# A fused four-layer graph kernel: four engines issue in the order of emission

## The chip, the cores and the metric

The kernel runs on one core of a Trainium2 chip, in fp32. Times are device microseconds from the start to the end of one launch. Three runs of the kernel before gave 2439.32, 2439.52 and 2441.19 us; the median is 2439.52 us. Lower is better.

## What is computed

The input x holds 128 graphs of 64 nodes with 256 features, and all share one 64 x 64 adjacency. Four layers follow each other, each with a residual and a layer norm:

```python
x = _layernorm(x + _L0_gnn_ref(x, adj, ...))   # A_hat x, 256->512, batch norm, relu, 512->256, batch norm
x = _layernorm(x + _L1_gnn_ref(x, adj, adj, ...))
x = _layernorm(x + _L2_gnn_ref(x, adj, ...))
x = _layernorm(x + _L3_gnn_ref(x, adj, W, a))  # graph attention: softmax over masked scores, times x W
```

Layer 0's two batch norms run over all 8192 rows, so nothing behind one can start before all rows are through what is ahead of it. Layer 1 is a Chebyshev step whose Laplacian is scaled by its largest eigenvalue, then a masked attention with 4 heads and an MLP with an exact gelu, with three affine layer norms. Layer 2 is two graph convolutions, then an LSTM over windows of 1, 2, 3 and 4 nodes, each rewriting some nodes of h:

```python
for p in range(1, MAX_SKIP + 1):
    wins = h[:, :nw * p, :].reshape(Bv * nw, p, Hd)
    last = _lstm_last(Wih[p - 1], Whh[p - 1], bih[p - 1], bhh[p - 1], wins)
    h = h.at[:, idx, :].set(last.reshape(Bv, nw, Hd))
```

## The kernel before, in words

**Tiles.** x is cut into 16 blocks of 8 graphs. A block is 4 tiles of 128 rows by 256 features, 128 x 1024 fp32. For each block there is one buffer with rows on the partitions (X[i]; x0 to x7 hold two blocks each) and one with features on the partitions (H[i]; h0 to h3 hold four each). Eight temporary buffers of a block's size (t0 to t7) and four PSUM buffers of two banks each (ps0 to ps3) are handed out and taken back by two stocks, `mem` and `PS`.

**The order of emission.** The kernel has a planner of its own, `flow` (L130). Each task is a Python generator which, ahead of every piece of work, yields the engine it needs and an estimate of its time ("T" for TensorE 3.45 us, "V" for VectorE 1.25, "S" for ScalarE 1.05, "G" for POOL 1.0, "Q" for a DMA), with the PSUM and temporary buffers it takes. `flow` keeps a model clock for each engine, picks the step that can start earliest, with margins and priorities of streams, and lets that task emit its instructions. So the order in which the program is written down is already a plan of the whole run. A step emits all its instructions together: the four tiles of a norm's statistics (L272, L273 for each tile, L274), or the eight operations of an affine norm's application (L297, L300 for each tile).

**The order of issue.** The program is written under a framework that tracks the tiles' dependencies, puts in the semaphores, and schedules: before the change, its scheduler is free to put each engine's instructions into another order than the one emitted, as long as dependencies hold.

**The stages.** The first `flow` runs layer 0: `first_block` (aggregation L322, L346, PSUM out L537, statistics), the batch norm's coefficients `bn_coeffs`, `second_block` (relu on ScalarE, L566, statistics), and beside them the largest eigenvalue by squaring a matrix again and again (L440 to L490; L468 is the squaring). Between the two flows stands set-up code: loads of weights on SP's queue (L855, L372, L862, and L381 for the biases bih and bhh), memsets on POOL, and on VectorE L870 and L873, `V.tensor_tensor(bl, bl, bh, ALU.add)`. The second `flow` (L1574) runs everything else in streams:
- `end_block` (L628 to L649), the end of layer 0: load of x on SP (L635), batch norm on ScalarE (L638), transposes on PE (L340, 128 x 128 each), residual from PSUM on VectorE (L646), layer norm. `ln_steps_act` (L301 to L316) does this norm: L272 to L274 on VectorE, the power -0.5 on POOL (L308), L311 on VectorE, then four L314 on ScalarE.
- `block`, layer 1: aggregation (L322), ScalarE copy L660, product with Wc (L358), PSUM out L669, an affine norm (`ln_affine_steps`, L286 to L300, with its power at L294), relu and residual L673, transposes L334, ScalarE copy L681, products L346 for q and k, the attention (VectorE L743 to L754, ScalarE L750) and the MLP.
- `gcn_block` and `lstm`, layer 2: L952 and L1024 are products on PE, L964 and L1104 gates from PSUM on ScalarE, L991 tanh on ScalarE, L983 and L830 products and sums on POOL, L1062 to L1100 moves and sums, L1222 to L1250 the graph convolution's evictions and relu.
- `last_block`, layer 3: L1364 copies on ScalarE, L1404, L1428, L1441 exponentials, L1450 to L1471 the weighted sums, L1161 to L1193 the last LSTM pieces beside them.

The streams overlap: block by block, layer 2 starts while layer 1 is under way, and layer 3 while layer 2's LSTM ends.

Of the kernel before, what the change touches and what calls it, by code (L numbers as in the profile page):

```python
# [33 lines left out]
def kernel(ctx: ExitStack, tc: tile.TileContext, a: dict, out: bass.AP):  # L34
    nc = tc.nc
    V, S, G, T = nc.vector, nc.scalar, nc.gpsimd, nc.tensor

    def bc_mid(ap, n):

        return ap.unsqueeze(1).to_broadcast([ap.shape[0], n, ap.shape[1]])  # L40
# [1595 lines left out]
```

## Time and profile before

| | |
|---|---|
| median of 3 runs | 2439.52 us (2439.32 to 2441.19) |
| the profiled execution | 2439.17 us |
| its span (first to last instruction) | 2437.4 us |
| granted TensorE clock, mean | 0.983 |
| DMA: bytes moved, share of 16 engines on the main queue | 57.47 MB, 6.9% |

A profile comes from one execution. PE is TensorE's matmuls, PEld its weight loads, DVE VectorE, ACT ScalarE, POOL GpSimd, SP the engine that issues the transfers (SPq in the lists). The page gives each engine's busy time first, then the span in 40 slices, a digit for the busy tenths of each; PEclk is the clock that the throttle granted PE, in tenths of full speed. Lists of waits name the waiting instruction, then the releaser: "PE ps L334 <- DVE t L673" is a matmul of line 334 into a PSUM buffer that waited for VectorE's line 673. In a timeline a line is: start, duration (both in us), engine, line, operation, output<-input, and in brackets the engine's idle time ahead of it with its releaser. In windows each engine's busy time in a stretch is followed by its number of instructions in brackets, then the mean clock, DMA share and GB/s. Lines are those of the kernel before.

### The profile page before, as it was taken

To read this page: it belongs to the slowest core of one execution; us is meant where nothing else is said; L and a number is where in the kernel's file an instruction comes from. 1 tells how busy PE (TensorE), PEld (TensorE's weight loads), DVE (VectorE), ACT (ScalarE), POOL (GpSimd) and SP (SyncE) were. 2 spreads that over 40 slices of the span, in tenths; PEclk is the share of its full clock that TensorE was granted. 3 is DMA by queue.
4 is the path that set the end of the run, shared out by engine and by line. 5 is a ranking of instruction groups with operands and counts; after the bars stand their busy time and mean duration, and the time that the engine had idled before them with its cause. 6 is when DMAs were issued, how large, how long until landed. Compare 5 with 4: busy or idle time off the path is not lost. (4 is left out here: it accounts for less than half of the span.)

```text
span 2437.4 us, 33965 instructions
## 1 busy us (share of the span) xinstructions
PE 2348.3 (96%) x13700; PEld 1798.9 (74%) x13700; DVE 1215.1 (50%) x2864; ACT 1169.9 (48%) x2138; POOL 566.7 (23%) x426
## 2 busy tenths in 40 slices
PE   8999889999999999999999999999999999998997
PEld 5544567766676666676676788899999888887785
DVE  4542377646475345744462433344435444455446
ACT  2255453543444444335544444444444654468766
POOL 0000034222333222422231221222212222122112
PEclk9999989999999999999999999999999999999998
DMA  5110111000000000000010000000001000001111
GB/s 172 44 52 0 40 31 49 27 9 10 1 10 18 10 9 10 1 10 34 20 61 1 18 1 1 1 18 1 1 1 35 1 9 10 18 27 66 40 35 44
DMA packets 40974, 57.47 MB, mean 24 GB/s; under 512 B 4592, under 2 KB 33904, under 8 KB 40816
## 3 DMA queue, kind: packets, MB, share of 16 engines
q1 hardware_dynamic: 39712, 54.22, 6.9%
q8 instruction: 107, 1.75, 0.3%
q10 hardware_dynamic: 1104, 1.08, 0.1%
q14 instruction: 51, 0.42, 0.1%
HBM read 38.52 MB, written 16.78 MB: 23 GB/s over the span
## 5 line engine op out<-in xcount | busy, mean ns | idle before, releaser
L1024 PE MATMUL ps<-x,x 128*128 128x256 f32 x1024 | 248.6, 380 | 0.7 <-DVE t L1092 0.7
L1024 PEld LDWEIGHTS ps<-x,x 128*128 128x128 f32 x1024 | 191.5, 190 | 26.4 <-issue 1.6
L314 ACT ACTIVATE x<-x,ln_nm,ln_rs 128x256 f32<-128x256 f32 x196 | 103.7, 592 | 97.0 <-DVE ln_nm L311 95.5
L1024 PE MATMUL ps<-t,x 128*128 128x256 f32 x576 | 141.0, 379 | 0.0
L308 POOL TENSOR_TENSOR ln_rs<-ln_rs,neghalf 128x4 f32<-128x4 f32 (+1 forms) x72 | 70.5, 980 | 231.1 <-DVE ln_rs L274 217.3
L1024 PEld LDWEIGHTS ps<-t,x 128*128 128x128 f32 x576 | 108.6, 190 | 14.6 <-issue 0.4
L346 PE MATMUL ps<-t,W1T 128*128 128x512 f32 x256 | 115.2, 593 | 0.0
L952 PE MATMUL ps<-h,wL 128*128 128x192 f32 (+2 forms) x504 | 111.6, 375 | 0.0
L952 PEld LDWEIGHTS ps<-h,wL 128*128 128x128 f32 x504 | 79.1, 190 | 27.6 <-issue 26.7
L272 DVE BATCH_NORM_STATS2 ln_st<-x 128x6 f32<-128x256 f32 x256 | 98.2, 404 | 0.5
L1100 ACT ACTIVATE t<-t,bih 128x512 f32<-128x512 f32 (+2 forms) x63 | 41.0, 652 | 107.6 <-DVE t L1090 105.9
L952 PE MATMUL ps<-h,x 128*128 128x256 f32 x384 | 86.8, 379 | 0.0
L964 ACT ACTIVATE t<-ps,bih 128x512 f32<-128x512 f32 (+3 forms) x104 | 61.5, 642 | 44.0 <-PE ps L952 43.9
L294 POOL TENSOR_TENSOR ln_rs<-ln_rs,neghalf 128x4 f32<-128x4 f32 x32 | 36.9, 1153 | 188.8 <-DVE ln_rs L274 188.6
L346 PEld LDWEIGHTS ps<-t,W1T 128*128 128x128 f32 x256 | 46.3, 190 | 46.4 <-issue 46.4
L952 PEld LDWEIGHTS ps<-h,x 128*128 128x128 f32 x384 | 72.9, 190 | 10.3 <-issue 0.5
L1083 DVE COPY t<-ps 128x256 f32<-128x256 f32 (+2 forms) x63 | 23.7, 378 | 113.5 <-PE ps L1024 113.5
L273 DVE BATCH_NORM_AGGREGATE ln_mv<-ln_st 128x2 f32<-128x6 f32 x448 | 71.3, 167 | 0.0
L346 PE MATMUL ps<-t,wA 128*128 128x512 f32 x144 | 67.9, 617 | 2.8 <-ACT t L681 2.8
L952 PE MATMUL ps<-t,wL 128*128 128x512 f32 x144 | 64.9, 607 | 2.5 <-ACT t L1250 2.5
L1090 DVE TENSOR_TENSOR t<-ps,t 128x512 f32<-128x512 f32 (+2 forms) x63 | 38.1, 604 | 54.8 <-PE ps L1024 47.9
L1100 ACT ACTIVATE x<-x,bih 128x512 f32<-128x512 f32 (+2 forms) x57 | 36.6, 641 | 55.7 <-DVE x L1090 55.4
(692 smaller groups left out, 5688.2 us busy)
## 6 DMA issues: line engine op xcount, KB each, us to landing
t<-in_x_dram SPq DMA_DIRECT2D x26, 512.0 KB, 3.9
xd<-x SPq DMA_DIRECT2D x16, 512.0 KB, 2.6
x<-xd SPq DMA_DIRECT2D x6, 512.0 KB, 3.3
out_dram<-x SPq DMA_DIRECT2D x6, 512.0 KB, 3.0
wL<-in_L_gnn_Wih_dram SPq DMA_DIRECT2D x2, 1024.0 KB, 4.9
h<-in_x_dram SPq DMA_DIRECT2D x4, 512.0 KB, 4.2
x<-in_L_gnn_Whh_dram SPq DMA_DIRECT2D x2, 1024.0 KB, 4.9
t<-xd SPq DMA_DIRECT2D x4, 512.0 KB, 3.3
```

Of the source, the lines that this page charges most:

```text
L272: V.bn_stats(st[:, t, :], y[:, t, :])
L273: V.bn_aggr(mv[:, t, :], st[:, t, :])
L294: G.tensor_tensor(rs, rs, neghalf[:, :NT], ALU.pow)
L308: G.tensor_tensor(rs, rs, neghalf[:, :n], ALU.pow)
L314: S.activation(y[:, t, :], y[:, t, :], AF.Identity, scale=rs[:, t : t + 1], bias=nm[:, t : t + 1])
L346: T.matmul(ps[:, c, :], w[:, k, (off + c) * P : (off + c + 1) * P], yT[:, k, :], start=(k == 0), stop=(k == nk - 1),)
L952: T.matmul(spread(fm(PS[ps])[:, j, :n], q), WL[p][0][:, k, m], x_of(0, q)[:, k], start=(k == 0), stop=(k == 1),)
L964: S.activation(of(sl)[:, j], fm(PS[ps])[:, j, :n], AF.Tanh if g == 2 else AF.Sigmoid, bias=bias(g, c))
L1024: T.matmul(dst, WS[p][name](k, g), y[:, k], start=first and k == 0, stop=k == 1, skip_group_check=not first)
L1083: V.tensor_copy(y[:, 1, :], v[:, 0, :])
L1090: V.tensor_tensor(y[:, 0:2, :], v[:, 2:4, :], y[:, 0:2, :], ALU.add)
L1100: S.activation(of(act[g])[:, 0], of(act[g])[:, 0], f, bias=bias(g, 0))
```

## The change

Two lines are put at the head of the kernel's function. They tell the framework that TensorE, VectorE, ScalarE and POOL issue their instructions in the order in which the program emits them. The transfers on SP's queue, and what the engines wait for among each other, stay with the framework. No instruction of the kernel's own is added, removed or altered, and `flow` emits the same order as before. In the kernel after, all lines stand two lower.

```diff
     nc = tc.nc
     V, S, G, T = nc.vector, nc.scalar, nc.gpsimd, nc.tensor
+    E = mybir.EngineType
+    ctx.enter_context(tc.manual_schedule(engines={E.PE, E.DVE, E.Activation, E.Pool}))
```

The built programs hold 69 loads of ScalarE's function table after the change and 73 before; these loads are put in by the compiler, where the function set of two successive activations differs.

## The prediction

> **What bounds the kernel now.** I read the busy times first, then the slices and the windows by stage, then PE's waits, then the timeline of single waits.
>
> ```profile
> PE 2348.3 (96%) x13700; PEld 1798.9 (74%) x13700; DVE 1215.1 (50%) x2864; ACT 1169.9 (48%) x2138; POOL 566.7 (23%) x426
> PE   8999889999999999999999999999999999998997
> PEclk9999989999999999999999999999999999999998
> ```
>
> PE is the bound, and its work is untouched. So only what PE loses can move: idle time (2437.4 - 2348.3 = 89 us, of which some 16 lie before its first and after its last matmul) and time at a lower clock. DVE and ACT at half of the span have slack on average. By stage (columns: length, then busy PE, PEld, DVE, ACT, POOL, granted clock):
>
> ```profile
> 150.00:350.00 200.00, 176.07 (x681) 95.30 (x681) 86.54 (x240) 116.35 (x174) 23.86 (x21) 0.92 0.07 20
> 500.00:600.00 100.00, 92.74 (x531) 64.83 (x530) 59.80 (x140) 40.73 (x57) 28.92 (x19) 0.93 0.03 11
> 960.00:1120.00 160.00, 150.95 (x1108) 107.26 (x1107) 100.00 (x213) 62.59 (x76) 57.36 (x32) 0.97 0.03 11
> 1200.00:1650.00 450.00, 449.92 (x2114) 371.44 (x2110) 192.85 (x359) 195.80 (x374) 108.45 (x74) 1.00 0.04 14
> 2180.00:2310.00 130.00, 116.53 (x767) 96.54 (x766) 75.24 (x253) 107.81 (x242) 25.44 (x28) 0.98 0.19 62
> 2380.00:2437.40 57.40, 40.28 (x276) 30.20 (x268) 33.92 (x150) 39.90 (x102) 13.04 (x20) 0.82 0.14 47
> ```
>
> From 1200 to 1650 nothing can be won: PE is busy throughout. The losses are single gaps in the other stages. The waits view (total, times, longest) names them; most occur once:
>
> ```profile
> PE ps L334 <- DVE t L673: 5.4, 1, 5.4
> PE ps L358 <- ACT h L964: 3.5, 1, 3.5
> PE ps L334 <- DVE t L1222: 3.4, 1, 3.4
> PE ps L340 <- ACT h L964: 3.4, 1, 3.4
> PE ps L346 <- ACT t L681: 2.8, 1, 2.8
> PE ps L952 <- ACT t L1250: 2.5, 1, 2.5
> ```
>
> A wait that names ACT L964 need not mean that ACT was slow. The timeline of ACT before the 3.4 us gap:
>
> ```profile
> 516.92 1.09 ACT L314 ACTIVATE x<-x,ln_nm,ln_rs 128x256 f32<-128x256 f32 x2 [4.30 <-DVE ln_nm L311]
> 517.92 0.61 ACT L991 ACTIVATE t<-h 128x512 f32<-128x512 f32 x1
> 518.44 1.08 ACT L314 ACTIVATE x<-x,ln_nm,ln_rs 128x256 f32<-128x256 f32 x2
> 519.42 1.24 ACT L964 ACTIVATE h<-ps,bih 128x512 f32<-128x512 f32 x2
> ```
>
> L964's input, PE's gate product, was finished at 514.73. ACT sat idle for 4.30 us, because an L314 that waited for a layer norm on DVE stood in front. The scheduler's order cost the gap, not ACT's speed. The granted clock is 0.50 from 519.47 to 526.30, just behind it.
>
> **What the skill says of it.** The Trainium skill, "TensorE: Matmul & The Clock Gate", table under "Why this matters for your kernels": PE gaps above some 3 us drop the clock to half; its section "What's actually happening" gives a window of 3.41 us that runs freely. The trace has the half-speed stretches in that unit (6.83 us behind 517.35 and 582.18, 3.41 behind 987.58, 1011.95 and 1096.3), but already behind a gap of 2.35 us, and none behind 1.75. I go by the trace: a removed gap of 2 us or more also pays back half of its stretch. The same skill, "PSUM — Partial Sum Buffer", "Engine vs sequencer instructions": ScalarE's, VectorE's and GpSimd's queues are strictly first in, first out. The ACT lines above agree, and the whole forecast rests on it: who stands in front decides.
>
> **The change, part by part.** It adds and removes no arithmetic. It fixes the order of four engines as the planner emits it; SP's 130 transfers stay with the scheduler. The two orders compared: PE keeps 6737 of 7236 instructions in place, DVE 959 of 2864, ACT 652 of 2077, POOL 107 of 431, SP 118 of 132. Four ACT table loads go (73 to 69; 1.28 us each in the chain of waits). All sums are against the profiled 2439.17 us (span 2437.4 and 1.8 around it), 0.35 below the median of 2439.52, which I ignore.
>
> 1. *Middle, 345 to 1200.* I followed each PE gap back through its releasers and asked which link the new order keeps. PE's own order there is unchanged. In each large case the instruction PE waits for was ready in time and no longer has the blocker in front:
> - 517.35 (3.37 us, above): L964 now ahead of L314.
> - 582.18 (3.47): L964 was ready at 578.64 but stood behind a tanh L991, which waited for POOL L983 behind POOL L830 (2.35 us).
> - 783.9 (1.61) and 892.2 (1.16): L1250 and L964 stood behind four L314 each.
> - 987.58 (3.42): DVE L1222 was ready at 984.54, behind L669 and L753 (1.22 us each) and a norm's statistics.
> - 1011.95 (2.53): DVE L1242 was ready at 1005.63, behind an affine norm.
> - 1093.5 and 1096.3 (0.76, 2.35): ACT L681 was ready at 1092.6, behind five L314.
> Sum 18.7 us, and small ones 2.4: 21.1. Half-speed stretches 2 x 6.83 + 3 x 3.41 = 23.9, half of that 11.9. Together 33. What takes a gap's place is the next-late operand, so I take 85%: **-28** (range -33 to -15).
>
> 2. *DVE in strict order, everywhere.* Step by step emission puts a consumer right behind its producer: 287 such neighbours before, 982 after (448 are L272 then L273, 128 are L297 then L300). In the trace a dependent neighbour costs 0.12 to 0.14 us more from start to start than an independent one (L273 0.22 against 0.08, L297 0.52 against 0.37). 695 x 0.125 = 87 us more on DVE, spread over a span where it idles 1220. This costs where DVE is dense: 650 to 700 goes from 43 to 48 of 50 us, 950 to 1000 from 46 to 51. There, and where the chain is a single norm (+0.5 us for stats, 3.2 to 3.9 for the eight affine operations), I take **+5** (0 to +15). Elsewhere PE's slack covers it: for each instruction that stands behind one it stood ahead of before, I compared its lateness with its slack to PE's use. From 345 to 1340 none is late beyond its slack by 0.4 us; from 1340 to 1990 only some seven are, by 0.4 to 1.1.
>
> 3. *Start of layer 1, 276 to 340.* In the old order the scheduler starts the second flow's work before the set-up that is emitted ahead of it; now DVE L873 (bl + bh) stands ahead of the first L646:
>
> ```profile
> 285.05 1.22 DVE L646 TENSOR_TENSOR x<-ps,t 128x1024 f32<-128x1024 f32 x1 [1.33 <-PE ps L340]
> 294.71 0.18 DVE L873 TENSOR_TENSOR bih<-bih,bhh 128x32 f32<-128x32 f32 x1
> 286.84 0.45 SPq L381 DMA_DIRECT2D bhh<-in_L_gnn_bhh_dram  x1
> ```
>
> bhh is issued at 286.84 behind six loads on SP's queue and lands 4.7 us later, at 291.5. All of DVE waits for that: +6.5 us on the first L646, and PE's second L340 with it. PE also loses the h3 transposes that the scheduler had pulled ahead as filler, and ACT does eight L314 before the L638 of h3. Followed by hand, PE reaches L334 of t6 at 320.7 instead of 313.65 (+7), and L346 of t7 at 341.7 instead of 337.28, since the gaps of 2.44 and 2.77 us at 331 and 334 mostly go. **+4.4** (0 to +10: a longer gap also stretches the half clock, 6.83 us behind 308).
>
> 4. *Small places.* First batch norm: one L468 moves ahead of L566, +0.8. From 1994 to 2002 the fillers move behind the chain L1450, L1452, L1460, L1471: +2.5; small gaps in 1663 to 2146 (4.4 in all), half gone: -2. SP's swaps cost nothing, as its DMA share is 3 to 7% there; without that cover, one landing (about 4 us). POOL's new order is costed within each chain.
>
> 5. *2186 to 2310.* ACT is dense (107.8 of 130). L1364 copies (1.07 us) and two table loads leave the chain at 2220 to 2232: -3.9; 2247: -1; 2305, with L1441 no longer split by two table loads: -1.9 and -1.7 for its half-speed stretch; 2189 +0.7. About **-7** with rounding down (-11 to -3).
>
> 6. *Tail, from 2398.* Two L1364 copies that feed L340 now stand behind L314 ready at 2406.8 and 2408.9, 3 to 4.6 us late beyond their slack; the gaps at 2399 and 2407 (2.8 each) partly overlap with it: **+2.5** (0.5 to 4.5).
>
> Sum: 0.8 + 4.4 - 28 + 5 + 0.5 - 7 + 2.5 = -21.8. Forecast **2417 us**, 0.991 of before.
>
> **The rivals.**
> - *All of it is recovered* (0.16): every middle gap closes (-33), DVE costs nothing, layer 1 starts without loss, 2186 to 2310 gives 9: about -40, **2399**. For it: PE streams once ahead. Against: the L873 wait is certain.
> - *The change does hardly anything* (0.12): PE's order is 93% the same and moves of DVE and ACT lie in slack; each removed gap reappears at the next operand. **2438**. Against: the six waits above are each broken at a named link.
> - *Strict order makes PSUM evictions late* (0.12, slower): a layer-1 eviction (L669, L646; 1.22 us) that used to slip between the parts of a norm must now wait out a whole affine step on DVE, 8 x 0.49 = 3.9 us. There are 32 such steps. If 1.5 us of each shows on PE, +48: 2417 + 48 = **2465**. It decides from 22 / 32 = 0.7 us per step. For it: DVE at 950 to 1000 would be full. Against: the comparison of lateness and slack under 2.
> - The forecast itself: 0.60, own range 2405 to 2431.
>
> **Numbers.** Differences under 0.2% (4.9 us) can't be told from none. Range 2399 to 2440: the forecast, full recovery and no change; the slow rival is left out. Faster 0.75, same 0.12, slower 0.13.
>
> **What would show it.** Right: PE's waits on L964, L1222, L1250 and L681 gone, clock 1.00 in 500 to 600 and 960 to 1120, PE's first L334 some 7 us later, DVE's busy time about 1300 us. Wrong: DVE at 50 of 50 us with PE waiting for L669 or L646 in 650 to 700 and 950 to 1000, or a gap beyond 12 us at 285 to 320.

## The result and the profile after

The kernel after takes 2467.35 us (median of 4 runs, 2466.93 to 2469.02), the kernel before 2439.42 in the same session (4 runs): ratio 1.0114, 95% interval 1.0097 to 1.0132. It is 27.9 us slower; the forecast was 22 us faster, and its range ended at 2440.

The head of the page of the kernel after (its lines stand two lower than before's):

```profile
span 2465.5 us, 34025 instructions
PE 2349.2 (95%) x13700; PEld 1800.0 (73%) x13700; DVE 1309.6 (53%) x2864; ACT 1156.1 (47%) x2134; POOL 567.0 (23%) x426
PE   9999789999999999999999999999999989998996
PEclk9999899999999999999999999999999999999998
```

PE's work is the same to 1 us, so all of the loss is idle time. VectorE has 94 us more (87 were forecast); ScalarE 14 us less.

**Where it went.** Both kernels run the same 13700 matmuls. I weigh each by the median interval to the next one's start, by line and shape in the trace of before, and compare the clocks at which the two have done equal work. This is the lag, in us (negative: ahead of before), along before's clock. The second row is what the lag gains over each stretch, and the third what the steps of the forecast say for it:

| | at 265 | 347 | 504 | 1206 | 1606 | 1858 | 2067 | 2170 | 2296 | end |
|---|---|---|---|---|---|---|---|---|---|---|
| after | 1.2 | 4.0 | 9.7 | -6.1 | -4.6 | 4.8 | 20.3 | 26.9 | 30.3 | 26.1 |
| stretch, measured | +1.2 | +2.8 | +5.7 | -15.8 | +1.5 | +9.4 | +15.5 | +6.6 | +3.4 | -4.2 |
| stretch, forecast | +0.8 | +4.4 | -23 from 347 to 1206 | | 0 | +0.5 from 1606 to 2170 | | | -7 | +2.5 |

(The lag is good to about 1 us, as the order of the matmuls differs by a few and some records are missing. It ends at the last matmul; the spans differ by 28.1 us.) The start is as forecast. The middle gives 10 us instead of 23. And from 1606 to 2170, where before lost hardly anything, after loses 31.5 us. PE's waits there, before first (total, times, longest; cut to 1600 to 2240):

```profile
PE ps L1450 <- ACT t L1104: 2.5, 1, 2.5
PE ps L1404 <- DVE ln_st L272: 1.8, 1, 1.8
PE ps L334 <- ACT h L1104: 1.7, 1, 1.7
PE ps L334 <- ACT t L1452: 1.2, 1, 1.2
PE ps L1024 <- ACT t L1104: 1.4, 2, 0.9
```

and after:

```profile
PE ps L1026 <- ACT t L1106: 4.6, 6, 1.3
PE ps L1452 <- ACT t L1106: 4.3, 3, 3.1
PE ps L1026 <- DVE t L1094: 3.8, 6, 1.8
PE ps L1026 <- DVE x L1094: 3.4, 4, 2.0
PE ps L1026 <- ACT x L1106: 3.1, 5, 1.3
PE ps L1026 <- ACT x L1418: 2.6, 1, 2.6
PE ps L1026 <- ACT h L1106: 2.4, 3, 1.3
```

Before has 11 gaps of PE over 0.3 us from 1600 to 2240, after 33. Most are of 0.5 to 2 us, and the commonest form is an LSTM product (L1026) that waits until ScalarE or VectorE has taken an earlier product out of PSUM (L1106, L1094): 17.9 of the 33.7 us of waits in this stretch. One place shows what PE's order has to do with it. Before (PE's timeline, start and length first):

```profile
1996.13 0.68 PE L1450 MATMUL ps<-ident,x 64*64 64x64 f32 x16
1996.74 0.70 PE L1024 MATMUL ps<-x,x 128*128 128x256 f32 x2
1997.28 0.59 PE L1024 MATMUL ps<-h,x 128*128 128x256 f32 x2
1997.80 0.68 PE L1450 MATMUL ps<-ident,x 64*64 64x64 f32 x16
1998.41 0.70 PE L1024 MATMUL ps<-h,x 128*128 128x256 f32 x2
1998.95 0.59 PE L1024 MATMUL ps<-x,x 128*128 128x256 f32 x2
1999.47 1.09 PE L1460 MATMUL ps<-t,x 64*64 64x256 f32 x16
```

and the same work after:

```profile
2006.03 0.68 PE L1452 MATMUL ps<-ident,x 64*64 64x64 f32 x16 [0.56 <-ACT t L1106]
2007.18 0.68 PE L1452 MATMUL ps<-ident,x 64*64 64x64 f32 x16 [0.47 <-ACT x L1454]
2008.33 1.09 PE L1462 MATMUL ps<-t,x 64*64 64x256 f32 x16 [0.47 <-ACT x L1454]
2010.91 1.13 PE L1026 MATMUL ps<-h,wB 128*128 128x256 f32 x4 [1.48 <-DVE x L1473]
```

The scheduler had put four pairs of LSTM matmuls between the steps of a chain in which each waits for an eviction; in the order of emission the chain runs bare, with a gap of 0.5 to 1.5 us at each link.

### The profile page after: what moved, and what is told of

The parts are those of the page before. It is cut to its first block, busy times and chain, and to the rows that moved or that the text cites. A ratio compares the mean times of both kernels' runs of the same rounds, so it can differ in the third digit from the quotient of the medians.

```text
span 2465.5 us, 34025 instructions
## 1 busy us (share of the span) xinstructions
PE 2349.2 (95%) x13700; PEld 1800.0 (73%) x13700; DVE 1309.6 (53%) x2864; ACT 1156.1 (47%) x2134; POOL 567.0 (23%) x426
## 5 line engine op out<-in xcount | busy, mean ns | idle before, releaser
L1026 PE MATMUL ps<-x,x 128*128 128x256 f32 x1024 | 248.2, 380 | 1.9 <-DVE x L1094 1.1
L1026 PEld LDWEIGHTS ps<-x,x 128*128 128x128 f32 x1024 | 191.6, 190 | 28.4 <-DVE x L1094 1.9
L1026 PE MATMUL ps<-t,x 128*128 128x256 f32 x576 | 140.2, 379 | 0.6 <-DVE h L1094 0.3
L1026 PEld LDWEIGHTS ps<-t,x 128*128 128x128 f32 x576 | 108.7, 190 | 15.4 <-issue 0.7
L274 DVE BATCH_NORM_STATS2 ln_st<-x 128x6 f32<-128x256 f32 x256 | 102.6, 401 | 0.6
L275 DVE BATCH_NORM_AGGREGATE ln_mv<-ln_st 128x2 f32<-128x6 f32 x448 | 81.5, 182 | 15.3
L966 ACT ACTIVATE x<-ps,bih 128x512 f32<-128x512 f32 (+3 forms) x80 | 47.2, 642 | 71.7 <-PE ps L954 71.7
L1064 ACT COPY t<-ps 128x256 f32<-128x256 f32 (+2 forms) x63 | 21.3, 338 | 104.0 <-PE ps L1026 100.4
L1085 DVE COPY x<-ps 128x256 f32<-128x256 f32 (+2 forms) x57 | 21.1, 371 | 80.3 <-PE ps L1026 80.1
```

The lines of the kernel that those rows point to most:

```text
L274: V.bn_stats(st[:, t, :], y[:, t, :])
L275: V.bn_aggr(mv[:, t, :], st[:, t, :])
L966: S.activation(of(sl)[:, j], fm(PS[ps])[:, j, :n], AF.Tanh if g == 2 else AF.Sigmoid, bias=bias(g, c))
L1026: T.matmul(dst, WS[p][name](k, g), y[:, k], start=first and k == 0, stop=k == 1, skip_group_check=not first)
L1085: V.tensor_copy(y[:, 1, :], v[:, 0, :])
```

## The experiments

My theory A: PE only shows the loss, and ScalarE's and VectorE's fixed order makes the evictions late (a ready sigmoid stands behind copies that wait for PE). Theory B: PE's fixed order is the cause. Theory C: VectorE's 94 us more. Times below are medians; "before" is 2439.7 to 2440.3 in each session. All edits are to the two lines of the change unless shown.

**One engine at a time**

```diff
-    ctx.enter_context(tc.manual_schedule(engines={E.PE, E.DVE, E.Activation, E.Pool}))
+    ctx.enter_context(tc.manual_schedule(engines={E.PE}))           # e1_only_pe
+    ctx.enter_context(tc.manual_schedule(engines={E.DVE}))          # e2_only_dve
+    ctx.enter_context(tc.manual_schedule(engines={E.Activation}))   # e3_only_act
```

> TensorE alone issues in the order of emission; VectorE, ScalarE and POOL stay with the scheduler. Theory A (evictions on ScalarE and VectorE stand behind instructions that wait): PE's own order costs little, 2438 to 2446 us, and no run of 1.3 us waits on ScalarE's line 1106 from 1600 to 2240. Theory B (PE's order, without the fillers that the scheduler had pulled ahead, costs the 28 us): 2460 us or more. Theory C (94 us more of VectorE by dependent neighbours cost it): about 2439, as VectorE stays at some 1215 us.

Measured 2460.14 us, 1.0084 (1.0067 to 1.0100): +20.0 against before.

> VectorE alone issues in the order of emission. Theory A: the waits on line 1094 behind cell sums and norm pieces are there (7 us), the middle gaps that VectorE's order caused (988, 1012) are gone (about 9 us with their half clock): 2436 to 2446 us. Theory B: about 2439. Theory C: 2460 us or more, VectorE's busy time about 1310 us.

Measured 2445.51 us, 1.0024 (1.0015 to 1.0034): +5.3, VectorE 1270 us busy.

> ScalarE alone issues in the order of emission. Theory A: ScalarE's waits on line 1106 from 1600 to 2240 are there (about 14 us of gaps), and the middle gaps at 517, 582, 784 and 892 are gone (about 16 us with their half clock): 2434 to 2446 us. Theory B and C: 2439 or less, and the 1106 waits of 1.3 us are absent, since they would come from PE's or VectorE's order.

Measured 2408.80 us, 0.9873 (0.9858 to 0.9888): **-31.4**. Windows of this kernel, for those of before shown with the forecast:

```profile
500.00:600.00 100.00, 100.00 (x589) 68.31 (x588) 63.37 (x146) 47.09 (x63) 35.98 (x21) 1.00 0.03 12
960.00:1120.00 160.00, 153.23 (x1104) 107.68 (x1104) 93.22 (x189) 63.84 (x76) 52.19 (x29) 0.98 0.02 8
```

The gaps at 517 and 582 and their half-speed stretches are gone (PE busy 100 of 100 us), without a late loss. Theory A falls for ScalarE. PE alone (e1) gives most of the late loss, as B says: 24.7 us by the lag from 1606 to 2170. C alone doesn't give it.

**Groups of engines**

```diff
+    ctx.enter_context(tc.manual_schedule(engines={E.DVE, E.Activation, E.Pool}))  # e5_no_pe
+    ctx.enter_context(tc.manual_schedule(engines={E.PE, E.Activation}))           # e6_pe_act
+    ctx.enter_context(tc.manual_schedule(engines={E.Activation, E.Pool}))         # e8_act_pool
```

> VectorE, ScalarE and POOL issue in the order of emission; TensorE is left to the scheduler. Theory B (the late loss of some 25 us from 1600 to 2240 comes from PE's fixed order, which can't go around an eviction that is late): that loss is gone, about 2467 - 23 = 2444 us or less, down to 2414 if ScalarE's gain of 31 us is then whole. Theory A (the evictions themselves are late because ScalarE's and VectorE's orders are fixed): the loss stays, 2460 us or more, with waits on lines 1106 and 1094.

Measured 2440.46 us, 0.9999 (0.9990 to 1.0008).

> TensorE and ScalarE issue in the order of emission. Theory B: the late loss is there without VectorE's order, and ScalarE's gain of the middle too: 2409 + 20 to 2409 + 25 = 2429 to 2434 us. Theory A with VectorE as the culprit: about 2409 to 2415, as VectorE is free to be in time.

Measured 2435.69 us, 0.9980 (0.9971 to 0.9990), 1.7 us above what B said.

> ScalarE and POOL issue in the order of emission. If POOL's order adds nothing of its own, 2406 to 2412 us as with ScalarE alone; if POOL's products and powers stood in wrong places, some us less; if its strict order makes norms late, up to 2425.

Measured 2418.34 us, 0.9910 (0.9895 to 0.9924).

Differences to before, one engine added at a time: ScalarE -31.4; POOL with it -22.0, so +9.4; VectorE too +0.1, so +22.1; PE too +27.9, so +27.8. PE's order costs 20.0 alone, 26.7 beside ScalarE's, 27.8 beside all. VectorE's costs 5.3 alone and 22.1 beside ScalarE's and POOL's.

**Part of the run.** e4 closes the region for all engines when the last block of layer 1 is emitted (about 1270 us), e9 for PE alone, e16 opens one for PE alone there.

```diff
+    man = ctx.enter_context(ExitStack())
+    man.enter_context(tc.manual_schedule(engines={...}))
...
         mark("l1", i)
+        if all(("l1", j) in done for j in range(NBLK)):
+            man.close()
```

> All four engines issue in the order of emission until the last block of layer 1 is emitted (about 1270 us of the run); from there on the scheduler orders all. Theory A: the trace after is 5 us ahead of before at that point and loses 31 us later, so 2431 to 2437 us, below before. Theory B: some 2439 if PE's order loses its time late. Theory C: VectorE is densest in the first half, so most of the loss would stay: 2455 us or more.

Measured 2437.04 us, 0.9987 (0.9980 to 0.9994): at the edge of what A said, and B's number is within 2 us of it, so it tells less than I meant it to; C falls.

> As the kernel after, but TensorE's order is fixed only until the last block of layer 1 is emitted; from there on the scheduler orders TensorE, and the other three stay in the order of emission. Theory B (PE's fixed order of the LSTM's products loses 25 us late): 2438 to 2446 us. Theory A (late evictions by ScalarE's and VectorE's fixed order): 2460 us or more.

Measured 2440.19 us, 1.0001 (0.9993 to 1.0010): +0.2, 27.7 us better than after. PE's waits on L1106 and L1094 (here L1110 and L1098) in 1600 to 2240 fall from 24.0 us in all to 6.8, and the longest waits there are now:

```profile
PE ps L1030 <- ACT t L1070: 2.4, 2, 1.6
PE ps L1456 <- ACT t L1110: 2.3, 1, 2.3
PE ps L1030 <- DVE t L1098: 1.8, 1, 1.8
```

> The kernel before, with TensorE alone in the order of emission, and only for what is emitted behind the last block of layer 1. If the late loss is TensorE's order of the LSTM and layer-3 products alone: 2440 + 20 to 25 = 2460 to 2465 us. If it needs the other engines' fixed orders too: 2438 to 2448 us.

Measured 2465.85 us, 1.0103 (1.0088 to 1.0118): +26.1. PE's order behind layer 1 makes the loss with nothing else fixed (22.2 us by the lag from 1606 to 2170), and without it the loss is mostly gone (e9: 7.2 of the 31.5 us are left). Theory B is shown for some 24 of the 31.5 us. The 7 that stay with PE free (7.3 in e5) belong to the orders of the other three together, as ScalarE's with POOL's costs 1.3 there (e8) and VectorE's alone 1.1 (e2); they are not traced further.

**VectorE's neighbours and its wait**

```diff
         for t in range(n):
             V.bn_stats(st[:, t, :], y[:, t, :])
-            V.bn_aggr(mv[:, t, :], st[:, t, :])
+            if t:
+                V.bn_aggr(mv[:, t - 1, :], st[:, t - 1, :])
+        V.bn_aggr(mv[:, n - 1, :], st[:, n - 1, :])
```

This and the same for the affine pairs is e11; e10 moves one line:

```diff
-    V.tensor_tensor(bl, bl, bh, ALU.add)
     def gcn_rows():
         yield step("Q", 4.0, sl=1)
+        V.tensor_tensor(bl, bl, bh, ALU.add)
```

> As the kernel after, but the sum of the two biases (before line 873, after line 875) is emitted in the task that loads layer 2's rows, some 60 us later, instead of ahead of the second flow. Nothing is left out. If its wait for the bias load costs what the trace shows (PE idle 8.0 us at the first line 648), the start of layer 1 gets 5 to 8 us shorter: 2459 to 2463 us. If the next wait (the 6.3 us on line 675, the norm behind it) takes over: 2464 to 2468 us.

Measured 2461.39 us, 1.0082 (1.0067 to 1.0097): +21.4, so 6.5 us better than after. VectorE's timeline of the kernel after shows the wait that goes:

```profile
292.79 0.19 DVE L875 TENSOR_TENSOR bih<-bih,bhh 128x32 f32<-128x32 f32 x1 [7.77 <-DMA bhh<-in_L_gnn_bhh_dram]
292.90 1.22 DVE L648 TENSOR_TENSOR x<-ps,t 128x1024 f32<-128x1024 f32 x1
```

> As the kernel after, but each norm's operations are emitted so that no VectorE instruction stands directly behind the one it needs: statistics of tile t+1 ahead of the aggregation of tile t, first affine operation of tile t+1 ahead of the second of tile t. If dependent neighbours cost what the forecast took (0.125 us each), VectorE's busy time falls from 1310 to about 1230 us, and the time by the forecast's term of 5 us (2460 to 2465); if denser VectorE is a large part of what its order costs, by 10 us or more (2457 or less); if none, 2466 to 2468.

Measured 2442.84 us, 1.0010 (1.0003 to 1.0017): +2.8, so **25.1 us** better than after, far beyond the term of 5. VectorE's busy time falls from 1309.6 to 1258.2 us. A norm in the kernel after,

```profile
418.43 0.42 DVE L274 BATCH_NORM_STATS2 ln_st<-x 128x6 f32<-128x256 f32 x1
418.89 0.18 DVE L275 BATCH_NORM_AGGREGATE ln_mv<-ln_st 128x2 f32<-128x6 f32 x1
418.99 0.39 DVE L274 BATCH_NORM_STATS2 ln_st<-x 128x6 f32<-128x256 f32 x1
```

and the same work in e11:

```profile
414.46 0.39 DVE L274 BATCH_NORM_STATS2 ln_st<-x 128x6 f32<-128x256 f32 x1
414.77 0.16 DVE L276 BATCH_NORM_AGGREGATE ln_mv<-ln_st 128x2 f32<-128x6 f32 x1
414.85 0.39 DVE L274 BATCH_NORM_STATS2 ln_st<-x 128x6 f32<-128x256 f32 x1
```

From one statistics to the next it is 0.56 us against 0.39 (in the median of each trace 0.53 and 0.39). By the lag, e11 stands at 1.3 at 347, -25.9 at 1206 and 2.4 at the end: 17 of the 25 us come from the middle, and the late loss is still there. In the middle (345 to 1200) the kernel before has six gaps of PE over 1.5 us and five stretches at half clock. After has four gaps (3.56 us at 425.5, 2.56 at 532.3, 2.43 at 590.9, 3.54 at 789.8) and a half-clock stretch of 3.41 us at the end of each but the third. e11 has one gap, of 1.96 us, and no half-clock stretch.

**Two misses on the late mechanism.** Both keep after's order except for a few places of each LSTM product step.

```diff
                 at[g, "a"] = yield step("S", copy_us, at=t - us, waits=False)
+                if g == 1:
+                    sigmoids(2)      # e7: the two activations of gate 2 that are ready
                 S.copy(y[:, 0, :], v[:, 0, :])
```

> As the kernel after, but in the LSTM's product steps the two ScalarE activations of gate 2 (lines 1102 and 1104), which are ready 3 to 4 us before they run, are emitted ahead of the next gate's two copies (1064, 1066), which wait for PE. Nothing is left out; PE's and VectorE's orders are those of the kernel after. Theory A: the five waits of 1.2 to 1.3 us on line 1106 between 1920 and 2120 shrink to the eviction's own 0.5 us, and smaller ones too: 2458 to 2463 us. Theory B: PE, in its fixed order, meets the next late operand instead: 2464 to 2468 us.

Measured 2467.53 us, 1.0101 (1.0081 to 1.0121), four runs from 2459.31 to 2468.44. In its profile three of the five waits, of 1.25 to 1.29 us at 1923, 2026 and 2030, are 0.56 or 0.57 each; the two at 2058 and 2117 stay. The wait next to the first grows from 0.71 to 0.98 us. By the lag 1606 to 2170 costs 30.8 instead of 31.5 us, and nothing is left of it at the end.

```diff
                 product(g, "A12", h_u, v[:, 2, :])
+                if g == 1:
+                    for f in later:  # e13: the first products and copies of gate 3
+                        f()
```

> As the kernel after, but in each LSTM product step the first products of gate 3 (and the two ScalarE copies behind them), which need a PSUM buffer that an eviction has just to free, are emitted behind one product of gate 1 whose buffer is at hand. The planner's decisions and all work stay the same. If TensorE loses late because the next product in its order needs the buffer under eviction: the 1.3 us waits on line 1106 at about 2026, 2030 and the like shrink, 2455 to 2463 us. If the loss has another cause: 2465 to 2469 us.

Measured 2465.59 us, 1.0105 (1.0090 to 1.0120). It reached only the waits behind gate 2's eviction: the one of 1.29 us at 2030 became 0.43, the one of 0.56 at 2041 went; those behind other gates stayed, and new small ones came. In the built programs PE's two orders differ in 27 places between 1600 and 2240, by one to seven instructions for the most part. That PE's order makes most of the late loss is shown; which of the places matters how much stays open.

**Versions that beat both.** e12 joins e9, e10 and e11; e14 is e12 without POOL in the region; e15 has VectorE and ScalarE alone in it, with the two edits of e10 and e11.

> The three edits together: TensorE free after layer 1, the bias sum later, norms emitted in pairs. If the three costs add up: 2467 - 25 - 6 - 5 = 2431 us, between 2424 and 2438. If VectorE's order has costs of other kinds, it stays near 2440, as with TensorE free throughout.

Measured 2405.94 us, 0.9861 (0.9846 to 0.9876). The three gains add to 27.7 + 6.5 + 25.1 = 59.3 us; together they give 27.9 + 34.1 = 62.0. It is far below what I expected (2424 to 2438), as I had put e11's part at 5 us.

> The three edits of e12 (TensorE free after layer 1, bias sum later, norms in pairs), and POOL left to the scheduler. If POOL's order costs by itself (large sums placed right behind the powers, where VectorE's next instruction is stretched to their end): 2394 to 2402 us. If its cost came only together with the scheduler's VectorE order: 2404 to 2409 us, as e12.

Measured 2402.92 us, 0.9846 (0.9829 to 0.9862), between the two expectations.

> Only ScalarE and VectorE in the order of emission, with the bias sum later and the norms in pairs; TensorE and POOL left to the scheduler throughout. If TensorE's order gains nothing in the first half: as e14, within 3 us. If it holds some of the gain there: up to 10 us more.

Measured **2401.11 us**, 0.9838 (0.9824 to 0.9853), the best: 38.8 us below before. POOL's order costs 3 us here, not the 9 of e8; PE's order up to layer 1 is worth nothing (e15 is 1.8 us below e14).

The edits alone, and with ScalarE's order:

> The kernel before, with the bias sum later and the norms emitted in pairs, all engines left to the scheduler. If the scheduler already keeps dependent VectorE neighbours apart, nothing changes: 2436 to 2444 us. If the edits by themselves gave the gain: 2400 to 2415 us.

Measured 2437.47 us, 0.9989 (0.9983 to 0.9996): -2.3, with VectorE 1213.7 us busy against 1215.1 before. The scheduler keeps most dependent neighbours apart by itself.

> The two edits, and ScalarE alone in the order of emission. If VectorE's order adds a gain of its own once its neighbours are apart, this is slower than the 2401 us with both, up to 2409 as with ScalarE alone; if not, 2399 to 2403 us.

Measured 2408.01 us, 0.9869 (0.9852 to 0.9885): -31.7. So ScalarE's order gives most of e15's 38.8 us, and VectorE's 7.1 once its neighbours are apart.

## Why the prediction was wrong, step by step

1. *Middle, -28.* The mechanism was right, and so was the size: e11, where VectorE's neighbours are apart, gains 27.2 us between 347 and 1206; ScalarE's order alone gains 20.8 there. In the kernel after it shows as -10, since step 2 took the rest. (PE's order there is not quite unchanged, as I had written; fixed alone it gains 2.6 us in this stretch, e1. And the 2 us from which a gap was to bring a half-clock stretch are no sharp bound: in the kernel after there is none behind the gap of 2.43 us at 590.9, and one of 3.41 us behind 1.95 us at 1610.)

2. *VectorE denser, +5.* **This term was mis-sized**: 25.1 us by e11. VectorE's total was right (about 1300 forecast, 1309.6 measured) for reasons that were half wrong. Keeping the neighbours apart takes 51 us of it away (1309.6 - 1258.2), not 87. Some 40 us more come from instructions that are stretched beside POOL (last section). I priced it as density in two dense windows. But from 347 to 1206 VectorE is busy only 554 of 859 us in the kernel after (526 in e11), and the 17 us are lost there all the same, in gaps with half-clock stretches behind them. My reading is that the norms of layer 1 lie on chains that PE waits for, so that the delay of a chain counts and not the density. The comparison of lateness with slack, which was to cover this, used before's durations. It could not see that the durations change.

3. *Start of layer 1, +4.4.* Right in the net: +2.8 by the lag. VectorE waited 7.77 us for bhh, PE 8.0 us; L334 of t6 was reached at 321.80 (320.7 forecast). The wait costs more than that (6.5 us by e10), and ScalarE's order, which I had down as a cost here, gains 4.6 when it is fixed alone (e3).

4. *Small places, +0.5 from 1606 to 2170.* **This is the step that failed.** It measured +31.5 there. "PE keeps 6737 of 7236 instructions in place" made me cost PE's order at one cluster (2.5 us; the gaps of the chain shown above add to 3.0, and the lag grows by 8.4 from 1962 to 2014) and take the rest for slack. Of the 499 others some 350 stand between 1600 and 2240, and PE's order costs 20 to 28 us in every setting (e1, e6, e9, e16). By the table this step is 31 of the 50 us between forecast and result; the middle, where step 2 was too small, is 13. Windows before, and then after, for about the same work:

```profile
1600.00:2180.00 580.00, 575.02 (x3397) 530.53 (x3396) 271.75 (x581) 281.78 (x670) 132.13 (x103) 1.00 0.03 9
```

```profile
1600.00:2210.00 610.00, 579.55 (x3372) 530.41 (x3371) 275.85 (x587) 279.45 (x670) 130.72 (x103) 0.99 0.02 8
```

PE at 575 of 580 us, with an eviction between a product and the next one into the same buffer, means that other products stand between them. I took the full stretch for one with nothing to lose, and did not ask what it rested on.

5. *2186 to 2310, -7,* and 6. *tail, +2.5.* Measured +3.4 and -4.2; with PE free (e9) -1.0 and -2.8. Both are small, and both have the wrong sign.

The slow rival, at 2465 us, has the measured time but not the cause. It put the loss on evictions that wait out affine steps in layer 1. VectorE's order does cost in layer 1, but through dependent neighbours (e11), and the larger loss lies behind layer 1, in PE's order (e16). "The change does hardly anything" is what three engines in order give (e5): a gain of 31 by ScalarE, eaten by POOL and VectorE.

What was to show the forecast right: of the four waits named, those on L964 of 3.4 and 3.5 us are gone and L1222's is 1.5 us, but L1250's (L1252 now) is longer than before, 3.5 us, and L681's went from one of 2.8 us to two of 1.1. The clock is 1.00 in 960 to 1120 but 0.98 in 500 to 600:

```profile
500.00:600.00 100.00, 95.01 (x537) 65.95 (x537) 67.74 (x138) 42.79 (x59) 26.37 (x18) 0.98 0.03 11
960.00:1120.00 160.00, 158.50 (x1185) 112.60 (x1184) 110.44 (x225) 67.78 (x81) 55.48 (x32) 1.00 0.03 11
```

## What to carry to other kernels

An order is a choice for each engine: try fixing one engine at a time. Here ScalarE's fixed order is worth 31 us, and PE's costs 20 to 28 out of the same plan. On the engine that bounds the kernel, a stretch without idle time is no proof of slack: count what stands between a product and the next one that needs its eviction before the order is changed. On VectorE, emit an independent instruction between a small producer and its consumer.

## What the hardware showed beyond that

A very small instruction on VectorE can take as long as a large sum on POOL. VectorE's timeline of the kernel after,

```profile
420.68 0.17 DVE L276 TENSOR_SCALAR ln_rs<-ln_mv 128x4 f32<-128x4 f32 x1
421.97 2.29 DVE L313 SCALAR_TENSOR_TENSOR ln_nm<-ln_mv,ln_rs 128x4 f32<-128x4 f32 x1 [1.12 <-POOL ln_rs L310]
424.19 1.28 DVE L745 TENSOR_TENSOR t<-ps,cap 128x512 f32<-128x512 f32 x2
```

and POOL's:

```profile
420.93 1.01 POOL L310 TENSOR_TENSOR ln_rs<-ln_rs,neghalf 128x4 f32<-128x4 f32 x1 [5.45 <-DVE ln_rs L276]
421.91 2.34 POOL L832 TENSOR_TENSOR x<-x,rows 128x1024 f32<-128x1024 f32 x1
```

L313 handles 4 elements in each partition, and takes 0.16 us in the median. Here it ends with POOL's sum, which began 0.06 us ahead of it. All 14 of the 72 L313 in this trace that take over 0.7 us end within 0.03 us of a POOL instruction that began ahead of them (8 such in before, 8 in e3, 15 in e8). Behind the long L313 stood L745, for which PE waited 3.6 us. The Trainium skill, "SBUF — State Buffer", "Terms", says that VectorE and GpSimd share a pair of ports which one of them holds for its whole instruction, while the other is blocked; the trace agrees. POOL's fixed order puts its next large sum right behind the power whose result VectorE's next small instruction needs. I add up what VectorE's instructions take above the median of their line and shape, where that is over 0.5 us: 87.2 us before, 99.8 with ScalarE in order (e3), 119.1 with POOL too (e8), 127.3 after. In the trace after, 83 of these 84 instructions started while one of POOL was under way that ended before they did. VectorE's own order adds little to it: alone it gives 83.8 (e2).

The second is the price of a dependent neighbour. The Trainium skill, "VectorE: DVE Perf Modes", "The DRAIN you can't avoid", reports that eight copies with a semaphore after each take no longer than with one at the end. Here the step from a statistics instruction to the aggregation right behind it, L274 to L275 after and L274 to L276 in e11, is 0.46 us from start to start in the lines shown where the second needs the first, and 0.31 where it doesn't (medians 0.43 and 0.31). With this and the same edit to the affine pairs the time of the kernel changes by 25 us (e11). For such small dependent instructions the measurement decides.
